# Groups of four share q and k, a block of two scores, four attends and two scores, softmax written over q and k: one edit of a four-layer graph network on Trainium2

## The chip, the cores and the metric

The kernel runs on one core of one Trainium2 chip, all in 32-bit floats. The metric is the device time of one launch in microseconds (us). The engines are named as the profile names them: PE is the matrix engine (PEld its weight loads), DVE the vector engine, ACT the scalar engine, POOL the general-purpose engine, and SP the engine that issues most DMAs. Each engine runs its own instructions in the order in which they were written down.

## The reference

There are 128 independent graphs ("batches") of 128 nodes with 512 features each, one shared 128x128 adjacency, and four layers, each followed by a residual and a layer norm. Cut to what matters:

```python
x = layernorm(x + (adj @ x) @ W0 + bias0)                    # layer 0
h = x @ W1                                                   # layer 1
e = leaky_relu(s1[:, None] + s2[None, :]) * adj              # s1, s2: h times two vectors
x = layernorm(x + elu(softmax(e) @ h + beta * h))
pre = A[:, :, None, :] + (C - A)[:, :, :, None]              # layer 2: A = adj @ x, C = A + b
x = layernorm(x + max(relu(pre), axis=-1))
q, k, v = split(x @ w_qkv)                                   # layer 3: 8 heads of 64
attn = softmax(where(adj == 0, -inf, q @ k.T * 64**-0.5))
o = (attn @ v) @ w_proj + b_proj
x = layernorm(x + o + layernorm(o) * gamma + beta3)
```

## The kernel before, in words

All weights stay in SBUF. Every batch is one 128x512 tile `xb` (nodes on the partitions), changed in place from its load to its store, with 16 such tiles (`BUFS["x"]`).

**The planner.** The program text is not written engine by engine. Each batch is a Python generator (`batch(i)`), and so are the side jobs of a group; each asks with `use(engine, work, names)` for a stretch of an engine, with an estimated duration and the buffers it needs. `Plan.run` simulates the engines and always emits next the request that could start earliest; ties go to `follow`, then `urgent`, then the lower rank (the older batch). The order so found is each engine's order on the chip. Buffers are taken in rotation: PSUM has five banks `mm` and three banks `tr`.

**Layers 0 to 2** of a batch: `mixed` (L231) multiplies the tile by the adjacency and turns it at once (L236, into a `tr` bank), ACT copies it out (L246), `product` (L224, L228) multiplies by W0, DVE adds (L643), a layer norm follows, then two logits per node (L650); `attention1` builds the attention of layer 1 for two batches, a second `mixed` and `product` apply it, DVE and ACT do the ELU (L666 to L671); one product with the adjacency (L678) and a maximum (L681) do layer 2.

**Layer 3** goes by groups, here of `G = 2` batches. `features` (L608) turns the tile with a DVE transpose (L692) and a trip through DRAM, into the group's buffer `xT` (two of these). When both batches are there, `query_key` (L507) runs four times per group: it multiplies two 128-column pieces of the weights with the group's `xT`, 256 columns wide (L519), and ACT or DVE copies the two pieces into the group's buffer `qkT` (L527, L529; three of these). `values` (L593) multiplies for v, at a low rank (`i + LATER`).

`tiled` (L536) is the block in which PE changes its tiling. It is emitted when q and k of a group are complete and the softmax rows of the group before it have come back. It holds the *scores* of its own two batches (L554: per batch 16 matmuls that contract over 64 rows, two at a time on the two halves of the array) and then the *attends* of the group before (`attends`, L582: 16 matmuls per batch that write 64 columns each). It asks for four `mm` banks, two `tr` banks, two `pr` and two `oT` buffers at once. After it, `batch` adds the mask (L706, out of the `mm` banks into `pr`), takes the maximum (L713), the exponentials on ACT (L717), the division (L723, L724), a 32x32 transpose into `pt` (L727), and a trip through DRAM into a buffer `prT` (L252, L256), which the attends read. The attended result is copied to `oT` (L749), multiplied by w_proj (L765, shown as L228), and `usual` (L762) does the rest: bias (L769), two layer norms, store.

The last 8 batches (`TAIL`) don't use the common block: their scores are emitted one batch at a time and their attends by pairs. The last 8 batches (`AHEAD`) also have their ranks lowered by 8. Batches 125 and 126 use `late` (L786), which puts part of the layer norms on ACT and stores from ACT's queue. Batch 127 uses `last` (L820): two column halves of the projection in one `mm` bank (L831), then DVE (L852, L853), one add on POOL of the whole tile (L221), the two layer norms and two half stores.

At the start `adjacency` (L348) clears a tile on DVE and multiplies it nine times (L355), then waits for the adjacency to land and transposes it (L360).

Each 32-bit `nc.tensor.matmul` appears in the trace as two MATMUL instructions, so a `product` is eight of 512 columns; a `nc.tensor.transpose` appears as one.

Of the kernel before, what the change touches and what calls it, by code (L numbers as in the profile page):

```python
# [15 lines left out]
P = 128  # L16
D = 512
K = D // P
G = 2
# [11 lines left out]
    "x": 16, "yT": 4, "z": 2, "e": 2, "et": 1, "eT": 2, "ex": 2, "xT": 2, "v": 6, "qkT": 3,  # L31
    "pr": 2, "pt": 1, "xt": 2, "prT": 2, "oT": 2, "o": 2,
}
AHEAD = 8
TAIL = 8
# [10 lines left out]
class Plan:  # L46

# [37 lines left out]
    def step(self, r, value):  # L85

        for want in iter(lambda: r["chain"].send(value), None):
            if not isinstance(want, Event):
                r["want"] = want
                self.requests.append(r)  # L90
                return
            if want.left:
                want.chains.append(r)
                return
            r["ready"], value = max(r["ready"], want.at), None
# [31 lines left out]
def gnn_stack_kernel(  # L127
# [62 lines left out]
    def mean_rstd_act(src, total):  # L190

        yield use("DVE", 0.15, follow=True)
        nm = small.tile([P, 1], F32, name="nm")
        nc.vector.tensor_scalar(nm, total, -1.0 / D, None, op0=ALU.mult)
        b = yield use("ACT", 1.2, "yT")
        square = buf([P, D], "yT")
        var = small.tile([P, 1], F32, name="var")
        nc.scalar.activation(square, src, AF.Square, bias=nm, accum_out=var)  # L198
        give(b)
        ve = small.tile([P, 1], F32, name="ve")  # L200
        nc.scalar.activation(ve, var, AF.Identity, bias=eps, scale=1.0 / D)
        return nm, (yield from root(ve, follow=True))
# [14 lines left out]
    def pool_add(dst, other, event, after=None):  # L217
        if after:
            yield after
        yield use("POOL", 1.4)  # L220
        nc.gpsimd.tensor_tensor(dst, dst, other, op=ALU.add)  # L221
        done(event)
# [8 lines left out]
    def mixed(xb, nodes, first=False):  # L231
# [6 lines left out]
        if first:  # L238

            yield use("DVE", 0.35, late=0.0)  # L240
            nc.vector.tensor_copy(yT[:, : K // 2], p[:, : K // 2])  # L241
            yield use("ACT", 0.05, urgent=True)
            nc.scalar.copy(yT[:, K // 2 :], p[:, K // 2 :])
        else:
            yield use("ACT", 0.6, urgent=True)
            nc.scalar.copy(yT, p)  # L246
# [16 lines left out]
    eps = const.tile([P, 1], F32, name="eps")  # L263
    nc.gpsimd.memset(eps, EPS)
# [40 lines left out]
    def loads():  # L305
# [14 lines left out]
        slot = yield use("SP", 1.0, "pr")  # L320
        matrix(w1_sb, w1)
        a_sb = buf([P, H, P], "pr").rearrange("p (s k) f -> p s (k f)", s=2)
# [24 lines left out]

    def adjacency():  # L348

        yield use("DVE", 0.1)  # L350
        nc.vector.memset(maskb, 0.0)
        b0 = yield use("PE", 2.0, "tr")
        p = bank([P, K, P], "tr")
        for i in range(9):
            nc.tensor.matmul(p[:, i % K, :], maskb, maskb, start=True, stop=True)  # L355
        give(b0)
        yield adj_in
        b0 = yield use("PE", 0.3, "tr", late=0.2, urgent=True)
        p = bank([P, K, P], "tr")
        nc.tensor.transpose(p[:, 0, :], adj_sb, ident)  # L360
        yield use("DVE", 0.3)
        nc.vector.tensor_copy(adjT, p[:, 0, :])
        give(b0)
        done(adj_ready)
# [35 lines left out]
    class Group:  # L400


        def __init__(self):
            self.s = small.tile([P, G, 2], F32, name="s")
            self.logits = [Event(2) for _ in range(G // 2)]
            self.attention = [Event() for _ in range(G // 2)]
            self.turned, self.qk = Event(G), Event(K)
            self.rows, self.attended = ([Event() for _ in range(G)] for _ in range(2))
            self.scored = [Event() for _ in range(G)]
            self.heads, self.o, self.prT, self.sc = {}, {}, [], {}  # L410
# [7 lines left out]

    groups = {}

    def group(g):
        if g not in groups:
            groups[g] = Group()
            for h in range(G // 2):
                plan.start(attention1(groups[g], h), g * G + 2 * h - (AHEAD if g * G >= NB - AHEAD else 0))
            for n in range(K):
                plan.start(query_key(groups[g], n // 2 * 2 + K * (n % 2)), g * G + n / K - (AHEAD if g * G >= NB - AHEAD else 0))


            rank = g * G - (AHEAD if g * G >= NB - AHEAD else 0)  # L430
            if g * G < NB - TAIL:
                plan.start(tiled(groups[g], groups.get(g - 1)), rank)
            else:
                for b in range(G):
                    plan.start(tiled(groups[g], None, (b,)), rank)
            if g * G >= NB - TAIL - G:
                for bs in ((0, 1),) if g * G < NB - G else ((0,), (1,)):
                    plan.start(attend(groups[g], bs), rank)
# [68 lines left out]
    def query_key(gr, c):  # L507
# [3 lines left out]
        if gr.qkT is None:  # L511
            bp, gr.slot["qkT"] = got
            gr.qkT = buf([P, 2 * K, G * P], "qkT")
        else:
            bp = got
        p = bank([P, 2, G * P], "mm")
        for j in range(2):
            for k in range(K):
                nc.tensor.matmul(  # L519
                    p[:, j, :], wqkv_sb[:, k, (c + j) * P : (c + j + 1) * P], gr.xT[:, k, :],  # L520
                    start=(k == 0), stop=(k == K - 1),
                )
        gr.read("xT", G + K)
        yield use("ACT" if c < K else "DVE", 0.69, urgent=True)
        dst = gr.qkT[:, c : c + 2, :]
        if c < K:
            nc.scalar.mul(dst, p, HD**-0.5)  # L527
        else:
            nc.vector.tensor_copy(  # L529
                dst.rearrange("p j (b c r) -> p (j b) c r", b=G, c=Q),  # L530
                p.rearrange("p j (b r c) -> p (j b) c r", b=G, c=Q),
            )
# [3 lines left out]
    def tiled(gr, before, bs=range(G)):  # L536
        yield gr.qk
        if before:
            for b in range(G):
                yield before.rows[b]  # L540
        n = len(bs)
        got = yield use(
            "PE", 0.25 + 0.88 * n + (0.88 * G + 0.15 if before else 0),
            lambda: ("mm", "mm", "pr") * n + ("tr", "oT") * (G if before else 0),
            late=0.0, urgent=True,
        )

        for b in bs:
            ps_b = [bank([P, K, P], "mm") for _ in range(2)]
            nodes = slice(b * P, (b + 1) * P)  # L550
            for c in range(K):
                for j in range(2):
                    rws = slice(j * HD, (j + 1) * HD)
                    nc.tensor.matmul(  # L554
                        ps_b[j][:, c, :], gr.qkT[rws, c, nodes], gr.qkT[rws, K + c, nodes],
                        start=True, stop=True,
                    )
            gr.read("qkT", G)
            gr.sc[b] = ps_b, got[:3]
            got = got[3:]  # L560
        if before:
            attends(before, range(G), got)

        for k, b in enumerate(bs):
            done(gr.scored[b], 0.15 - 0.88 * (n - 1 - k) - (0.88 * G + 0.3 if before else 0.15))

    def attend(gr, bs):
        for b in bs:
            yield gr.rows[b]
        slots = yield use(  # L570
            "PE", 0.25 + 0.88 * len(bs), lambda: ("tr", "oT") * len(bs), late=0.0, urgent=True
        )
        attends(gr, bs, slots)

    def attends(gr, bs, slots):
        for n, b in enumerate(bs):
            valued, prT, bt = gr.heads.pop(b)
# [9 lines left out]
            give(bt)  # L587
            give(valued.slot)
            gr.o[b] = p, slots[2 * n], slots[2 * n + 1]
        for b in bs:  # L590
            done(gr.attended[b], 0.2)

    def values(i, gr, event):  # L593
        b = i % G
        yield gr.turned
        bp = yield use("PE", 3.46, "mm", late=0.2)
# [3 lines left out]
        bv = yield use("ACT", 0.6, "v", urgent=True)  # L600
# [3 lines left out]
        gr.read("xT", G + K)  # L604
# [21 lines left out]
    def batch(i):  # L626
        g, b = divmod(i, G)
        h = b // 2
        yield loaded[i]
        gr, xb = group(g), xs[i]  # L630
# [58 lines left out]

        bt = yield use("DVE", 0.71, "xt")  # L690
# [11 lines left out]
        bpr = slots[2]  # L702
        for j in range(2):
            yield use("DVE", 0.69, urgent=True)
            pr = pr if j else buf([P, H, P], "pr")
# [9 lines left out]
        for j in range(H):  # L715
# [14 lines left out]
        give(bpr)  # L730
# [4 lines left out]
        got = yield use("SP", 0.5, lambda: () if gr.prT else ("prT",) * G, late=4.0)  # L735
        gr.prT = gr.prT or got
        bt = gr.prT.pop()
        prT = buf([P, Q, H * S], "prT")
        from_rows(prT, scratch)
        prT = prT.rearrange("p a (h s) -> p h a s", h=H)  # L740

        yield valued
        gr.heads[b] = valued, prT, bt
        done(gr.rows[b])
        yield gr.attended[b]
        p, ba, bo = gr.o.pop(b)
        yield use("ACT", 0.6, urgent=True)
        oT = buf([P, K, P], "oT")
# [3 lines left out]
        yield from (last if i == NB - 1 else late if i >= NB - 3 else usual)(  # L752
            i, xb, oT, bo, biased
# [8 lines left out]
    def usual(i, xb, oT, b_oT, biased):  # L762
# [3 lines left out]
        give(b_oT)  # L766
        bo = yield use("DVE", 0.69, "o", urgent=True)
        o = buf([P, D], "o")
# [11 lines left out]
        give(bo)  # L780
# [5 lines left out]
    def late(i, xb, oT, b_oT, biased):  # L786

        bp = yield use("PE", 3.46, "mm", late=0.2)
        p = product(lambda k: oT[:, k, :], lambda k: wproj_sb[:, k, :])
        give(b_oT)  # L790
        bo = yield use("DVE", 0.77, "o", urgent=True)
        o = buf([P, D], "o")
# [135 lines left out]
```

## Time and profile before

| | |
|---|---|
| median of 3 runs | 3264.58 us (3263.59 to 3264.89) |
| the profiled execution's own time | 3264.25 us |
| its span, first to last instruction | 3262.2 us |
| PE | 14,627 MATMUL, 3248.3 us busy |
| DVE | 2637.5 us busy, 81% of the span |
| ACT, POOL | 36% and 29% |
| mean granted PE clock | 0.999 |

The span is cut by the profile into rows by source line. A row has a busy time, the mean duration of one instruction and the idle time of its engine just before it with its releaser. For PE the mean duration of one instruction (593 ns for 128x512) is longer than the distance between two, as they are pipelined; distances are read from the timeline, where a run of equal matmuls has a start and a count, and the next run's start ends it.

### The profile page before, as it was taken

The page shows a single profiled execution, that of the slowest core. Times are in us where ns is not written, and L with a number is a line of the kernel's source. Part 1 is how long each engine was busy: PE and PEld are TensorE (multiplying, and loading weights), DVE is VectorE, ACT ScalarE, POOL GpSimd, SP SyncE. Part 2 cuts the span into 40 slices and gives each one's busy share as a digit, 9 for nine tenths or more (in the row PEclk, how much of TensorE's full clock was granted, in tenths as well). Part 3 has the DMA queues.
Part 4 walks back from the last instruction along what each step waited for, and adds up shares of the span by engine and source line. Part 5 has one row for each costly group of instructions (what it writes and reads, how often), then busy time and mean ns, then how long its engine had stood idle before and what let it go on. Part 6 is the DMA issues. An engine that isn't in the chain of part 4 may idle for free.

```text
span 3262.2 us, 43758 instructions
## 1 busy us (share of the span) xinstructions
PE 3248.3 (100%) x14627; PEld 2064.6 (63%) x14627; DVE 2637.5 (81%) x5656; ACT 1187.4 (36%) x3471; POOL 960.8 (29%) x1032
## 2 busy tenths in 40 slices
PE   9999999999999999999999999999999999999998
PEld 5666666665666656666566666665666656666665
DVE  7888788888887888888878888788887888788776
ACT  2433334333343333433424333243333333333333
POOL 3323232322322323223232232223322232223212
PEclk9999999999999999999999999999999999999999
DMA  4323323333223323233232332323323233223332
GB/s 165 84 82 98 102 81 91 103 87 94 96 75 104 98 82 101 73 101 100 81 105 72 97 104 77 108 74 95 105 72 108 80 92 102 75 89 96 89 113 81
DMA packets 469904, 304.47 MB, mean 93 GB/s; under 512 B 319280, under 2 KB 401584, under 8 KB 469680
## 3 DMA queue, kind: packets, MB, share of 16 engines
q1 hardware_dynamic: 469248, 300.90, 30.6%
q8 instruction: 116, 1.90, 0.2%
q14 instruction: 108, 0.88, 0.1%
q10 hardware_dynamic: 432, 0.79, 0.1%
HBM read 158.93 MB, written 142.67 MB: 92 GB/s over the span
## 4 chain that ended last, share of the span: by engine, by line
PE 100%; DVE 0%; ACT 0%; issue 0%; POOLq 0%; POOL 0%; DVEq 0%
PE mm L228 54%; PE mm L519 27%; PE tr L236 7%; PE mm L554 4%; PE tr L582 4%; PE mm L678 3%; PE tr L355 0%; PE mm L831 0%; DVE ex L867 0%; PE tr L394 0%; DVE st L853 0%; ACT yT L198 0%; DVE o L852 0%; DVE x L806 0%; DVE ex L802 0%
## 5 line engine op out<-in xcount | busy, mean ns | idle before, releaser
L228 PE MATMUL mm<-w_sb,yT 128*128 128x512 f32 x2048 | 908.0, 593 | 0.5 <-DVE yT L241 0.5
L519 PE MATMUL mm<-xT,wqkv_sb 128*128 128x256 f32 x4096 | 898.6, 379 | 0.0
L187 POOL TENSOR_TENSOR rstd<-ve,neghalf 128x1 f32<-128x1 f32 x640 | 457.2, 715 | 1420.2 <-DVE ve L181 1167.7
L519 PEld LDWEIGHTS mm<-xT,wqkv_sb 128*128 128x128 f32 x4096 | 777.3, 190 | 137.7 <-issue 29.8
L228 PEld LDWEIGHTS mm<-w_sb,yT 128*128 128x128 f32 x2048 | 384.0, 190 | 455.8 <-issue 445.1
L228 PE MATMUL mm<-wqkv_sb,xT 128*128 128x512 f32 x1024 | 460.2, 593 | 0.0
L228 PE MATMUL mm<-wproj_sb,oT 128*128 128x512 f32 x1016 | 447.0, 592 | 0.0
L717 ACT ACTIVATE pr<-pr,nmx 128x128 f32<-128x128 f32 x1024 | 396.3, 389 | 42.5 <-DVE nmx L713 41.3
L173 DVE BATCH_NORM_STATS2 st<-x 128x6 f32<-128x512 f32 x509 | 347.4, 683 | 25.3 <-ACT x L686 21.8
L228 PEld LDWEIGHTS mm<-wproj_sb,oT 128*128 128x128 f32 x1016 | 191.9, 190 | 231.4 <-issue 224.6
L228 PEld LDWEIGHTS mm<-wqkv_sb,xT 128*128 128x128 f32 x1024 | 188.3, 190 | 206.5 <-issue 203.4
L527 ACT ACTIVATE qkT<-mm 128x512 f32<-128x512 f32 x128 | 76.4, 597 | 628.7 <-PE mm L519 628.7
L221 POOL TENSOR_TENSOR x<-x,bias_sb 128x512 f32<-128x512 f32 x128 | 166.0, 1303 | 439.2 <-PE tr L236 429.8
L246 ACT COPY yT<-tr 128x512 f32<-128x512 f32 x255 | 149.4, 586 | 286.1 <-PE tr L236 285.8
L210 ACT ACTIVATE x<-x,nmr,rstd 128x512 f32<-128x512 f32 x256 | 205.5, 807 | 124.4 <-DVE nmr L208 120.4
L221 POOL TENSOR_TENSOR x<-x,o 128x512 f32<-128x512 f32 x128 | 178.3, 1393 | 218.9 <-DVE o L769 213.5
L221 POOL TENSOR_TENSOR x<-x,beta_sb 128x512 f32<-128x512 f32 x128 | 166.2, 1300 | 218.2 <-DVE xt L692 215.7
L666 ACT ACTIVATE ex<-mm 128x512 f32<-128x512 f32 x128 | 76.2, 596 | 346.5 <-PE mm L228 345.8
L650 DVE SCALAR_TENSOR_TENSOR scr<-x,wa_rows 128x512 f32<-128x512 f32 x256 | 186.0, 727 | 15.6 <-ACT x L210 10.8
L717 ACT ACTIVATION_READ_ACCUMULATOR pr<-pr,nmx 128x1 f32 x1024 | 192.8, 188 | 0.0
L706 DVE TENSOR_TENSOR pr<-mm,maskb 128x512 f32<-128x512 f32 x256 | 162.0, 682 | 28.8 <-PE mm L554 28.8
L724 DVE TENSOR_TENSOR pr<-pr,rs 128x1024 f32<-128x1024 f32 x128 | 161.8, 1264 | 4.4
(89 smaller groups left out, 3499.4 us busy)
## 6 DMA issues: line engine op xcount, KB each, us to landing
p_d<-pt SPq DMA_DIRECT2D x128, 512.0 KB
prT<-p_d SPq DMA_DIRECT2D x128, 512.0 KB
x_d<-xt SPq DMA_DIRECT2D x128, 256.0 KB
xT<-x_d SPq DMA_DIRECT2D x512, 64.0 KB
x<-in_x SPq DMA_DIRECT2D x127, 256.0 KB
out<-x SPq DMA_DIRECT2D x125, 256.0 KB
z<-s_d SPq DMA_DIRECT2D x64, 128.0 KB
e_d<-et SPq DMA_DIRECT2D x64, 128.0 KB
```

Source lines behind the costliest of these rows:

```text
L173: nc.vector.bn_stats(st, src)
L187: nc.gpsimd.tensor_tensor(rstd, ve, neghalf, op=ALU.pow)
L210: nc.scalar.activation(xb, xb, AF.Identity, bias=nmr, scale=rstd)
L221: nc.gpsimd.tensor_tensor(dst, dst, other, op=ALU.add)
L228: nc.tensor.matmul(p, lhs(k), rhs(k), start=(k == 0), stop=(k == K - 1))
L236: nc.tensor.matmul(p[:, k, :], xb[:, k * P : (k + 1) * P], nodes, start=True, stop=True)
L246: nc.scalar.copy(yT, p)
L519: nc.tensor.matmul(p[:, j, :], wqkv_sb[:, k, (c + j) * P : (c + j + 1) * P], gr.xT[:, k, :], start=(k == 0), stop=(k == K - 1),)
L650: nc.vector.scalar_tensor_tensor(scr, xb, 1.0, wa_rows[:, j, :], op0=ALU.mult, op1=ALU.mult, accum_out=gr.s[:, b, j : j + 1],)
L706: nc.vector.tensor_tensor(pr[:, j * K : (j + 1) * K], sc[j], maskb[:, None, :].to_broadcast([P, K, P]), op=ALU.add,)
L717: nc.scalar.activation(pr[:, j, :], pr[:, j, :], AF.Exp, bias=nmx[:, j : j + 1], accum_out=sums[:, j : j + 1],)
L724: nc.vector.tensor_tensor(pr, pr, rs[:, :, None].to_broadcast([P, H, P]), op=ALU.mult)
```

## The change

- `G` becomes 4. The first 29 groups ("quads", batches 0 to 115) have four batches; the last twelve batches make six groups of two (`PAIRS = 6`). `query_key` on a quad runs eight times with one 128-column piece each, 512 columns wide; on a pair it stays as it was. `xT` and `qkT` are twice as large, with two of each.
- `tiled` on a quad emits the scores of two batches, the attends of the four batches of the quad before (three at once, as there are three `tr` banks, and the fourth behind them), and the scores of the other two. Pairs emit scores per batch and attends per pair.
- The buffers `pr`, `prT`, `oT` and `o` are gone. The masked scores and the softmax of a batch are written over its q and k in `qkT`, and so are the turned rows that come back from DRAM. The attended result and then `o` are written over v. `qkT` is given back after the group's attends, v after the last use of `o`. `x` has 18 tiles (was 16), `v` 8 (was 6).
- `values` takes its v buffer together with PE. `early(i)` lowers the ranks of the last 14 batches by 8 (`LAST = 14`).
- `late` is gone: batches 125 and 126 use `usual`. `last` puts its halves in two `mm` banks and adds them on POOL half by half.
- At the start, ten transposes of the identity take the place of the nine products of zeros, with two more after the adjacency's transpose and two more after the first `mixed`. The DVE clear is gone.

```diff
-G = 2
+G = 4
+PAIRS = 6
-    "x": 16, "yT": 4, "z": 2, "e": 2, "et": 1, "eT": 2, "ex": 2, "xT": 2, "v": 6, "qkT": 3,
-    "pr": 2, "pt": 1, "xt": 2, "prT": 2, "oT": 2, "o": 2,
+    "x": 18, "yT": 4, "z": 2, "e": 2, "et": 1, "eT": 2, "ex": 2, "xT": 2, "v": 8, "qkT": 2,
+    "pt": 1, "xt": 2,
-AHEAD = 8
-TAIL = 8
+LAST, AHEAD = 14, 8
...
+    def fill(n):
+        for i in range(n):
+            nc.tensor.transpose(idle[0][:, i % K, :], ident, ident)
     def adjacency():
-        yield use("DVE", 0.1)
-        nc.vector.memset(maskb, 0.0)
         b0 = yield use("PE", 2.0, "tr")
-        p = bank([P, K, P], "tr")
-        for i in range(9):
-            nc.tensor.matmul(p[:, i % K, :], maskb, maskb, start=True, stop=True)
-        give(b0)
+        idle.append(bank([P, K, P], "tr"))
+        fill(10)
...
     def query_key(gr, c):
-            gr.qkT = buf([P, 2 * K, G * P], "qkT")
+            gr.qkT = buf([P, G, 2 * K, P], "qkT")
-        p = bank([P, 2, G * P], "mm")
-        for j in range(2):
+        n = gr.chunks
+        p = bank([P, n, gr.size * P], "mm")
+        for j in range(n):
             for k in range(K):
                 nc.tensor.matmul(
-                    p[:, j, :], wqkv_sb[:, k, (c + j) * P : (c + j + 1) * P], gr.xT[:, k, :],
-                    start=(k == 0), stop=(k == K - 1),
+                    p[:, j, :], wqkv_sb[:, k, (c + j) * P : (c + j + 1) * P],
+                    gr.xT[:, k, : gr.size * P], start=(k == 0), stop=(k == K - 1),
                 )
...
-    def tiled(gr, before, bs=range(G)):
+    def tiled(gr, before, bs):
         yield gr.qk
+        waiting = list(range(before.size)) if before else []
+        for b in waiting:
+            yield before.rows[b]
+        for n in range(0, len(bs), 2):
+            now, then = bs[n : n + 2], waiting[: BUFS["tr"]]
+            got = yield use(
+                "PE", 0.1 + 0.88 * len(now) + 0.15 + 0.87 * len(then),
+                lambda: ("mm", "mm") * len(now) + ("tr",) * len(then),
+                late=0.0, urgent=True, follow=n > 0,
+            )
...
+            for b in now:
+                score(gr, b, got[:2])
+                got = got[2:]
+            if then:
+                attends(before, then, got)
...
+            waiting = waiting[len(then) :]
+            while waiting:
+                got = yield use("PE", 0.88, "tr", late=0.0, follow=True)
+                attends(before, waiting[:1], [got])
+                waiting = waiting[1:]
...
     def attends(gr, bs, slots):
-            give(bt)
-            give(valued.slot)
+            gr.read("qkT", gr.size)
...
     def values(i, gr, event):
-        bp = yield use("PE", 3.46, "mm", late=0.2)
+        bp, bv = yield use("PE", 3.46, lambda: ("mm", "v"), late=0.2)
...
+        pr = gr.qkT[:, b]
...
+        prT = pr.rearrange("p h n -> p (h n)")
+        from_rows(prT.rearrange("p (a f) -> p a f", a=Q), scratch)
...
+        oT = valued.v.rearrange("p (k n) -> p k n", k=K)
         nc.scalar.copy(oT, p)
...
-        yield from (last if i == NB - 1 else late if i >= NB - 3 else usual)(
+        yield from (last if i == NB - 1 else usual)(
...
+        def multiply():
+            for h, columns in enumerate(halves):
+                bp = yield use("PE", 1.73, "mm", late=0.0, follow=h > 0)
+                p = bank([P, D // 2], "mm")
...
+            nc.vector.tensor_tensor(o[:, columns], p, bproj_sb[:, columns], op=ALU.add)
+            nc.vector.bn_stats(st[:, h], o[:, columns])
+            give(bp)
+            plan.start(pool_add(xb[:, columns], o[:, columns], added, biased, 0.7), i)
```

## The prediction

> **What bounds the kernel now.** I read the page's totals first, then PE's waits, then the timeline around one `tiled` block, then both ends of the span.
>
> ```profile
> span 3262.2 us, 43758 instructions
> ...
> PE 3248.3 (100%) x14627; PEld 2064.6 (63%) x14627; DVE 2637.5 (81%) x5656; ACT 1187.4 (36%) x3471; POOL 960.8 (29%) x1032
> ```
>
> PE is never free. Its whole list of waits is three, 2.0 us, all in the first 8 us:
>
> ```profile
> PE tr L355 <- DVE maskb L351: 1.1, 1, 1.1
> PE mm L228 <- DVE yT L241: 0.5, 1, 0.5
> PE tr L236 <- DVE adjT L362: 0.4, 1, 0.4
> ```
>
> So the span is a head, the sum of the distances between PE's matmuls, and a drain after the last one (3250.1 us by start and distance). Only what changes one of the three counts. Distances come from the timeline (start us, busy us, instruction, count): the next run's start ends a run. First a usual block, then one near the end:
>
> ```profile
> 1009.85 3.60 PE L228 MATMUL mm<-w_sb,yT 128*128 128x512 f32 x8
> 1013.38 2.06 PE L554 MATMUL mm<-qkT 64*128 64x128 f32 x32
> 1015.36 1.97 PE L582 MATMUL tr<-prT,v 128*64 128x128 f32 x32
> 1017.26 2.05 PE L236 MATMUL tr<-adjT,x 128*128 128x128 f32 x16
> 1019.15 3.62 PE L519 MATMUL mm<-xT,wqkv_sb 128*128 128x256 f32 x16
> 1022.61 7.03 PE L228 MATMUL mm<-wproj_sb,oT 128*128 128x512 f32 x16
> 1029.47 10.52 PE L519 MATMUL mm<-xT,wqkv_sb 128*128 128x256 f32 x48
> ...
> 3203.81 3.60 PE L228 MATMUL mm<-wproj_sb,oT 128*128 128x512 f32 x8
> 3207.34 1.16 PE L554 MATMUL mm<-qkT 64*128 64x128 f32 x16
> 3208.43 1.97 PE L582 MATMUL tr<-prT,v 128*64 128x128 f32 x32
> 3210.33 1.16 PE L554 MATMUL mm<-qkT 64*128 64x128 f32 x16
> 3211.42 3.70 PE L228 MATMUL mm<-wqkv_sb,xT 128*128 128x512 f32 x8
> ```
>
> Two facts are in there. L228 goes at 429.2 ns per 512 columns (1022.61 to 1029.47 is 16 of them), and L519 at 215.8 ns per 256 (48 in 10.36 us over its run). And a change of tiling costs time: eight L228 take 3.43 us undisturbed but 3.53 before scores. Instruction by instruction the distances around the blocks are the same everywhere: into scores +0.094 on the last full matmul; a run of scores has 0.102 on its first pair (213 for 112 ns) and 0.097 on its last; a run of attends 0.050 and 0.100 on a pair of 109; the first full matmul afterwards +0.104. A block of two scores and two attends thus carries 0.547 us besides its matmuls. The second block above is already the new shape, scores-attends-scores, and carries 0.094+0.199+0.150+0.199+0.104 = 0.746.
>
> **The change, part by part.**
>
> *Fewer changes of tiling.* Before, by the order of PE's runs: 59 common blocks, 4 lone pairs of scores (0.397 each), 4 lone pairs of attends (0.348), one scores-attends-scores: 32.3+1.6+1.4+0.7 = 36.0 us. After: the first quad's four scores 0.4, 28 blocks of the new shape 20.9, the last quad's attends as two pairs 0.7, six groups of two at 0.745 each 4.5: 26.5. Gain 9.5 us. The twelve last batches in twos are dearer than quads, which is counted. Lone runs that meet (as in the second block) would add up to 1 us.
>
> *Query and key at 512 columns.* 116 batches lose 16 MATMULs each: 1856 pairs of 256 become one of 512, at 2x215.83-429.17 = 2.5 ns: gain 4.6 us. The products are the same size and the weight loads stay covered (190 ns of load per 429). ACT and DVE copy as many columns as before.
>
> *What moves off PE's path.* Mask, maximum, exponentials, division, transpose, both DRAM trips and the three DVE or ACT copies keep their sizes and engines; only the tile they write differs. I cost this at nothing: DVE is 81% busy under a PE that is 100% busy. Were that cover gone it would be paid in waits, next.
>
> *The waits that it adds.* (a) The fourth attend needs the `tr` bank of the first, which ACT must have copied out: `oT` takes 0.59 us on ACT (L749), and between the end of attend one and the start of attend four lie two attends, 1.75 us. With 0.3 us to get through PE and at most an ACT instruction in the way (0.81), it fits. Behind it in PE's order stand the last two scores, and everything else. (b) These need four of five `mm` banks, so three of the first four masked (L706, 0.682 each, 2.05 us) and the product before the block evicted (0.69): 2.74 us of DVE. It has from 1.2 us after the scores' start (in the block shown DVE's first mask began at 1014.57) to 5.5, where the attends end: 4.3 us. A DVE instruction under way (up to 1.26, the division) leaves 0.3. It fits, narrowly. (c) q and k of quad g+2 wait for the attends of quad g, as `qkT` now lives through the softmax and there are two. A quad is 3262.2/32 = 101.9 us of PE; its eight query-key products are 27.5 and the block 7.4, so 35 after the release it could score. (d) The rows of quad g must return in the same time: per batch DVE works 2x0.682+1.205+0.193+1.264+1.236 = 5.26 us, 21 for four; DVE does other work for 60% of the time, so 53 us, and in the trace rows follow their score by 25 us with one pair in flight, transfers included. (e) v is held to the end of `o`; outputs followed attends by 15 to 25 us, some 40 with four in a row, which leaves 60 for four values of 3.4. All under 102 us, and 18 instead of 16 batches in flight are 50 us more for the group's wait. So PE should stay full. What each would cost if late is below. On SP's queue nothing is added but two earlier loads and the stores of 125 and 126, which leave ACT's; the from-DRAM transfer no longer waits for a `prT` tile.
>
> *The head.* The real work starts when the adjacency lands:
>
> ```profile
> 1.05 4.16 PE L355 MATMUL tr<-maskb 128*128 128x128 f32 x18 [1.05 <-DVE maskb L351]
> 5.05 0.27 PE L360 MATMUL tr<-ident,adj_sb 128*128 128x128 f32 x1
> ```
>
> The 18 multiplications of zeros go at 213 ns, and what follows at 111: the full clock came 4.0 us after PE's first instruction, just in time. The ten transposes can start when the identity is there (POOL ends it at 1.33) and last 2.1 us, to 3.6, with a gap until 4.8.[...] By the row (4.0 us after whatever comes first) the change costs nothing.[...] No transposes at a cold PE stand in this trace. I take 0.8, as the gap makes even counted transposes weaker than the row's; ends 0 and 2.8.[...]
>
> *The drain.* It is 12.1 us, from 3250.1 to 3262.2:
>
> ```profile
> 3250.34 0.42 DVE L852 TENSOR_TENSOR o<-mm,bproj_sb 128x256 f32<-128x256 f32 x1 [2.63 <-PE mm L831]
> 3251.75 1.26 POOL L221 TENSOR_TENSOR x<-x,o 128x512 f32<-128x512 f32 x1 [1.85 <-DVE o L852]
> 3254.33 0.75 DVE L806 SCALAR_TENSOR_TENSOR x<-ex,rstd,x 128x512 f32<-128x512 f32 x1
> 3255.19 0.74 DVE L873 SCALAR_TENSOR_TENSOR x<-ex,rstd,x 128x512 f32<-128x512 f32 x1
> ```
>
> The first half's add waited for the whole bank; with two banks it and its statistics (0.9 us) go under the second half. The POOL add of the whole tile (1.26) stood before the root of batch 127; half of it will. Without batch 126's DVE work in between, L873 could start near 3252.5 instead of 3255.19: 2.7 us. But 126 on `usual` needs 4.8 us of DVE, where `late` needed 2.8, and it lands in the same stretch. I take 1.7, ends 0 and 2.7.
>
> **Sum** against the profiled execution: 3264.25-9.5-4.6+0.8-1.7 = 3249.3; that execution was 0.3 below the median, so 3249.6 us.
>
> **The rivals.**
> - *The block breaks up.* If the planner finds no bank for the fourth attend, or for the second scores, it puts a product in between: scores after a product instead of after attends cost 0.198 more, and attends in two runs 0.348. Over 28 blocks 5.5 or 9.7 us of the 14.1 go: 3255 to 3260. For it: all three `tr` and four of five `mm` are asked for. Against: (a) and (b). 10%.
> - *PE starves at the end.* The last twelve batches in twos have shorter chains of PE work to hide a softmax behind, and 125 and 126 lean on DVE. Before, PE had no wait there. 3 to 8 us: 3252 to 3258. 10%.
> - *Slower: the second scores stand in the block.* If DVE's masks come late, PE waits in order, once per quad. 14.1 us over 28 blocks is 0.50 us each: beyond this the gain is gone, and with a division and a transpose ahead of the evictions (1.26+1.24+2.74 = 5.2 in 4.3) it is 0.9 us, and the time 3249.6+25 = 3275. For it: DVE at 81%, and a burst of four outputs follows each block. Against: the 0.3 us of room in the usual case, and masks are urgent. 5%.
> - *The change doesn't do it*: if switches didn't depend on order, only 4.6 us and the drain would stay, 3259. The second block shown speaks against it. 2%.
>
> **How the numbers follow.** The forecast as above, with clock and drain at either end, 73%: 3246.5 to 3253. The rivals take the range to 3259; below 3246 nothing in the parts reaches. What a measurement can tell from no change is 0.2%, 6.5 us, so faster means below 3258. Slower than 3271 is the third rival alone. Faster 0.88, same 0.08, slower 0.04.
>
> **What would show it.** PE has 14627-1856-4 = 12767 MATMULs; L519's row splits into 1856 of 512 and 384 of 256 columns; the blocks read 32, 64, 32 in the timeline with 0.746 us besides; PE's waits stay a few us in the head; the first product's distances are 429 ns (or 853 if the clock is late); L852's first half starts before PE ends. If PE shows waits on L706 or L749, or many more than the 35 to 41 runs of scores followed by a full matmul that the new order has, I was wrong on the block; if they lie after 3100 us, on the end.

## The result, and the profile after

The changed kernel takes 3252.30 us (median of six runs, 3251.55 to 3252.77) against 3264.41 us: 12.1 us less, a ratio of 0.9963 (95% interval 0.9950 to 0.9976). The forecast was 3249.6. The profiled execution was the quickest of the six, 3251.55 us, with a span of 3249.8 us against 3262.2.

The totals on the changed kernel's page:

```profile
span 3249.8 us, 40319 instructions
...
PE 3233.9 (100%) x12767; PEld 1713.2 (53%) x12767; DVE 2669.2 (82%) x5671; ACT 1186.4 (37%) x3469; POOL 954.7 (29%) x1032
```

L535 from its groups kept apart by shape (busy us, mean ns of one, idle before):

```profile
L535 PE MATMUL mm<-xT,wqkv_sb 128*128 128x512 f32 x1856 | 804.1, 592 | 0.0
```

The counts are those forecast: 12,767 MATMULs, 1856 of them query-key products of 512 columns. PE's waits, the whole list (total us, times, longest):

```profile
PE tr L353 <- POOL ident masks.py:199: 1.4, 1, 1.4
PE mm L706 <- ACT x L211: 0.8, 1, 0.8
PE mm L824 <- ACT v L776: 0.7, 1, 0.7
PE mm L229 <- ACT v L776: 0.7, 1, 0.7
PE mm L229 <- DVE yT L243: 0.3, 1, 0.3
```

Three of them are new and lie behind the head. None is inside a block, on L735 (the masks) or on a `tr` bank. (The lines are those of the changed kernel: its L706 is layer 2's product with the adjacency, not the mask that was L706 before. Its L776 is the copy of the attended result, L749 before; the two waits on it lie at 3228 and 3233 us, and it is the product with w_proj that waits, not an attend.) The block, from PE's timeline (start us, busy us, instruction, count):

```profile
1032.42 2.06 PE L590 MATMUL mm<-qkT 64*128 64x128 f32 x32
1034.40 3.71 PE L611 MATMUL tr<-qkT,v 128*64 128x128 f32 x64
1038.05 2.06 PE L590 MATMUL mm<-qkT 64*128 64x128 f32 x32
1040.03 12.28 PE L229 MATMUL mm<-wproj_sb,v 128*128 128x512 f32 x28
```

Two scores, four attends, two scores, with nothing between; 28 blocks read so. The fourth attend never waits for its bank: the 64 MATMULs of the four attends take 3.65 us, and 64 times their plain distance of 54.6 ns is 3.49; the other 0.15 is the surcharge of the run's two edges.

Taken apart by the distances between PE's matmuls, the two profiled executions differ by 12.4 us of span. (A wait is counted here as the distance beyond the plain one, so 0.97, 0.95 and 0.95 us, where the list above has the idle time of 0.8, 0.7 and 0.7. The drain is counted from the start of the last matmul.)

| part | forecast | found |
|---|---|---|
| changes of tiling | -9.5 | -9.6 (35.7 to 26.1) |
| merged query-key products | -4.6 | -4.6 |
| head, up to the first product with W0 | +0.8 | -1.1 (7.38 to 6.29 us) |
| PE's waits behind the head | 0 | +2.9 |
| drain after the last matmul | -1.7 | 0.0 (12.33 both) |
| sum | -15.0 | -12.4 |

### The profile page after: what moved, and what is told of

It reads as the page before. It is cut to its first block, busy times and chain, and to the rows that moved or that the text cites. A ratio compares the mean times of both kernels' runs of the same rounds, so it can differ in the third digit from the quotient of the medians.

```text
span 3249.8 us, 40319 instructions
## 1 busy us (share of the span) xinstructions
PE 3233.9 (100%) x12767; PEld 1713.2 (53%) x12767; DVE 2669.2 (82%) x5671; ACT 1186.4 (37%) x3469; POOL 954.7 (29%) x1032
## 4 chain that ended last, share of the span: by engine, by line
PE 99%; DVE 1%; POOL 0%; issue 0%; ACT 0%; POOLq 0%; DVEq 0%; ACTq 0%
PE mm L229 54%; PE mm L535 27%; PE tr L237 7%; PE mm L590 4%; PE tr L611 4%; PE mm L706 3%; DVE st L177 0%; POOL rstd L191 0%; PE tr L353 0%; DVE x L805 0%; POOL x L222 0%; DVE t L802 0%; DVE x L699 0%; DVE mv L183 0%; DVE v L795 0%
## 5 line engine op out<-in xcount | busy, mean ns | idle before, releaser
L535 PE MATMUL mm<-xT,wqkv_sb 128*128 128x512 f32 (+1 forms) x2240 | 888.7, 556 | 0.0
L535 PEld LDWEIGHTS mm<-xT,wqkv_sb 128*128 128x128 f32 x2240 | 425.1, 190 | 455.6 <-issue 424.9
L229 PE MATMUL mm<-wproj_sb,v 128*128 128x512 f32 x1016 | 444.4, 594 | 0.7 <-ACT v L776 0.7
L746 ACT ACTIVATE qkT<-qkT,nmx 128x128 f32<-128x128 f32 x1024 | 395.4, 390 | 40.1 <-DVE nmx L742 40.1
L222 POOL TENSOR_TENSOR x<-x,v 128x512 f32<-128x512 f32 x127 | 175.9, 1385 | 671.3 <-DVE v L795 669.5
L229 PEld LDWEIGHTS mm<-wproj_sb,v 128*128 128x128 f32 x1016 | 191.2, 190 | 235.6 <-issue 230.3
L544 ACT ACTIVATE qkT<-mm 128x512 f32<-128x512 f32 (+1 forms) x140 | 77.1, 560 | 554.8 <-PE mm L535 553.6
L735 DVE TENSOR_TENSOR qkT<-mm,maskb 128x512 f32<-128x512 f32 x256 | 163.7, 684 | 78.6 <-PE mm L590 78.5
L746 ACT ACTIVATION_READ_ACCUMULATOR qkT<-qkT,nmx 128x1 f32 x1024 | 193.7, 189 | 0.0
L630 ACT COPY v<-mm 128x512 f32<-128x512 f32 x128 | 74.8, 585 | 297.0 <-PE mm L229 296.5
```

Source lines behind the costliest of these rows:

```text
L229: nc.tensor.matmul(p, lhs(k), rhs(k), start=(k == 0), stop=(k == K - 1))
L535: nc.tensor.matmul(p[:, j, :], wqkv_sb[:, k, (c + j) * P : (c + j + 1) * P], gr.xT[:, k, : gr.size * P], start=(k == 0), stop=(k == K - 1),)
L735: nc.vector.tensor_tensor(pr[:, j * K : (j + 1) * K], sc[j], maskb[:, None, :].to_broadcast([P, K, P]), op=ALU.add,)
L746: nc.scalar.activation(pr[:, j, :], pr[:, j, :], AF.Exp, bias=nmx[:, j : j + 1], accum_out=sums[:, j : j + 1],)
```

## The experiments

All times are medians of 4 to 12 runs; each is compared with the changed kernel's 3252.30 unless said otherwise. The kernel before, timed beside every experiment, kept a median of 3264.1 to 3264.4.

**The block taken apart (e1_split).**

```diff
-            now, then = bs[n : n + 2], waiting[: BUFS["tr"]]
+            now, then = bs[n : n + 2], waiting[:2]
+            if n:
+                apart = Event()
+                done(apart, 6.0)
+                yield apart
...
-                late=0.0, urgent=True, follow=n > 0,
+                late=0.0, urgent=True,
...
-            while waiting:
+            while waiting and n + 2 >= len(bs):
```

> The changed kernel with each quad's block taken apart: two scores and two attends, then at least six planned us of other work, then the other two scores and two attends. By the order of PE's runs that makes 56 blocks of two scores and two attends plus the loose runs of the two ends, 37.3 us of tiling changes against 26.4 in the changed kernel. Theory (the time is PE's distances, and the block's gain is the tiling changes it saves): 10.9 us more than the changed kernel's 3252.3, so 3263, all of it at the edges of L590 and L611 runs. Rival (the gain came from groups of four and the freed buffers, not from the order inside the block): 3252 to 3254.

Measured: 3267.74 us, 15.4 more. The timeline has the two blocks per quad, with two products between, and one place of another kind:

```profile
1035.40 2.06 PE L594 MATMUL mm<-qkT 64*128 64x128 f32 x32
1037.39 1.97 PE L615 MATMUL tr<-qkT,v 128*64 128x128 f32 x32
1039.29 3.70 PE L229 MATMUL mm<-w_sb,yT 128*128 128x512 f32 x8
...
3168.65 1.09 PE L615 MATMUL tr<-qkT,v 128*64 128x128 f32 x16 [2.27 <-DMA qkT<-p_d]
3169.68 5.40 PE L535 MATMUL mm<-xT,wqkv_sb 128*128 128x256 f32 x16
```

In the spans the difference is 16.5. Of this 5.5 are PE's waits near the end and what follows one of them (a wait of 2.3 us for softmax rows, after which PE lost its full clock: the 16 MATMULs at 3169.68 take 5.24 us instead of 3.45), 0.5 head and drain, and 10.5 the edges of the blocks, where 10.9 was worked out. The order inside the block is worth what the distances say; the rival (no loss at all) is out. The other 5.5 us were not expected.

**Query and key 256 wide (e2_qk256).**

```diff
-        n = gr.chunks
-        p = bank([P, n, gr.size * P], "mm")
+        n = 2
+        p = bank([P, n, 2 * P], "mm")
...
-                    gr.xT[:, k, : gr.size * P], start=(k == 0), stop=(k == K - 1),
+                    gr.xT[:, k, 2 * h * P : 2 * (h + 1) * P], start=(k == 0), stop=(k == K - 1),
...
-            dst = gr.qkT[:, : gr.size, c + j, :]
+            dst = gr.qkT[:, 2 * h : 2 * h + 2, c + j, :]
```

> The changed kernel with the quads' query-key products 256 columns wide again (two 128-column pieces for two batches at a time), everything else kept, block order too. Theory (2.5 ns for every matmul that is not merged, 1856 of them): 4.6 us more, 3256.9; L535 all at 215.8 ns. ACT and DVE copy in twice as many instructions, some 15 us more DVE work, which lies under PE. Rival 1 (the width is nothing, weight loads and matmuls overlap): 3252.3. Rival 2 (the extra DVE instructions are felt, DVE being 82% busy): over 3260 with PE waits on DVE.

Measured: 3257.64, 5.3 more. The 4096 matmuls are back at 215.8 ns, with the blocks in the same order. The span is 5.8 longer: 4.6 is the merging, 0.8 one new wait of PE for layer 1's attention from DRAM, 0.3 the head. DVE's additional instructions (116 of them, 7.7 us by the two pages, where 15 were expected) show in no wait of PE.

**The head: the old products of zeros (e3_old_head), and nothing at all (e4_no_warm).** The edits put back the clear and the nine products of the kernel before, or leave out all of `fill`.

> The changed kernel with the old start: nine products of zeros behind a DVE clear, no transposes of the identity. Theory (the 18 matmuls at 213 ns held back the adjacency's transpose, which had landed by 3.5 us, and the full clock came in time either way): the first product with W0 starts near 7.4 instead of 6.29 us, 1.1 us more, 3253.4. Rival (transposes don't count towards the full clock, so the old start is the better one): full clock earlier than 4.9 us and no later first product, 3252 or less.

> The changed kernel with nothing on PE before the adjacency lands: no transposes of the identity at all. Theory (the ten transposes counted towards the full clock, which came 3.5 us after the first of them): full clock comes 3.4 to 4 us after the adjacency's transpose, so near 7 to 7.5 us instead of 4.9; the first mixed takes 0.8 us more and part of the first product runs at 853 ns a matmul; first product some 0.8 us later and 0.5 to 1 us longer, 3254. Rival (transposes don't count, the clock follows the real products alone): full clock at 4.9 us as with them, 3252.3.

Measured: 3252.95 and 3254.78. The first differs from the changed kernel by less than the runs spread (3252.11 to 3254.17 against 3251.55 to 3252.77), so that only the traces tell the two starts apart; the second is clear of it (3254.01 to 3255.23). First the changed kernel's start, then that without any warm-up:

```profile
1.36 2.40 PE L353 MATMUL tr<-ident 128*128 128x128 f32 x10 [1.36 <-POOL ident masks.py:199]
3.55 0.47 PE L362 MATMUL tr<-ident,adj_sb 128*128 128x128 f32 x1
6.29 3.70 PE L229 MATMUL mm<-w_sb,yT 128*128 128x512 f32 x8 [0.30 <-DVE yT L243]
```

```profile
3.69 0.45 PE L357 MATMUL tr<-ident,adj_sb 128*128 128x128 f32 x1 [3.69 <-DMA adj_sb<-in_adj]
7.12 5.95 PE L229 MATMUL mm<-w_sb,yT 128*128 128x512 f32 x8 [0.52 <-DVE yT L241]
12.90 1.28 PE L237 MATMUL tr<-adjT,x 128*128 128x128 f32 x10
```

The adjacency lands by 3.7 us. In the kernel before its transpose stood behind 18 matmuls of zeros until 5.05. In the changed kernel the MATMULs of 128 columns start 213 ns apart up to 4.4 us and 111 ns apart from 4.9 us on, 3.5 after the first transpose. Without the transposes the first product takes 5.78 us instead of 3.54. If the 2.24 us more are a stretch at half clock, this lasts 4.5 us and ends near 11.6: my estimate from these two numbers, where I had expected the full clock at 7 to 7.5 (the expectation's 853 ns a matmul is an estimate too, four times the 213 ns that 128 columns took). By itself this is one profile each. e8_last_first, which has the same start, decides: its first multiplication of data is

```profile
4.45 1.16 PE L237 MATMUL tr<-adjT,x 128*128 128x128 f32 x8
```

Its eight MATMULs take 1.16 us, like those at 5.71 us in the kernel before, of which the last seven start 111 to 112 ns apart; in e4_no_warm, with a single transpose ahead of them, they take 2.08. PE had done nothing but thirteen transposes until then, so transposes do count towards the full clock here. With the old start the same eight took 1.64 us this time, and the first product started at 8.00. When the full clock comes differs from run to run: a second profile of the unaltered changed kernel (e12_after_again, below) has 2.08 us for these eight instead of 1.38, and its first product at 7.22 us instead of 6.29. All eleven profiles with the ten transposes have it between 6.13 and 7.22 us, the two with the old start at 7.38 and 8.00. The gain of the new start thus lies between 0.2 and 1.9 us; the table's 1.1 is one draw of each.

**The drain: 125 and 126 on ACT again (e5_late), and 127 ahead of 126 on DVE (e8_last_first).** The first puts back `late` with v's tile for o. The second adds three lines:

```diff
         mv, rstd = yield from mean_rstd(o)
+        if i == NB - 2:
+            yield measured
         yield added
...
         mv, ve = mean_var(st)
+        done(measured)
         rooted, rstd = beside(root(ve, follow=True), i)
```

> The changed kernel with batches 125 and 126 finished on ACT as before the change (the old function for them, with v's tile for o), 127 as in the changed kernel. Theory (127's first half was ready at 3236.1 but stood behind 126's layer norms on DVE until 3239.07; this is why the drain stayed at 12.3 us): with 2 us less DVE work of 126 in the way the drain shrinks by 1.5 to 2.5 us, 3250.3. Rival (the drain is bound by 127's own chain of DVE and POOL steps after the second half): no change, 3252.3.

> The changed kernel where batch 126's second step (the scaled o and everything behind it on DVE) is written down only after batch 127's statistics of o, so that on DVE both halves of 127 come before it. Nothing is added or left out. Theory (the drain stayed at 12.3 us because 127's first half stood behind 126's layer norm on DVE until 3239.07): the first half's add starts near 3237.3, and the drain is 1 to 1.7 us shorter, 3251.0. Rival (126's work only moves behind, and its store ends last): 3252.3 or more.

The drain of the changed kernel, from the timeline (batch 126's L805, then 127's first half):

```profile
3238.41 0.75 DVE L805 SCALAR_TENSOR_TENSOR x<-t,rstd,x 128x512 f32<-128x512 f32 x1 [0.44 <-POOL rstd L191]
3239.07 0.42 DVE L839 TENSOR_TENSOR yT<-mm,bproj_sb 128x256 f32<-128x256 f32 x1
```

PE's last matmul starts at 3237.4: the first half's add, meant to go under the second half's products, comes after all of them. In e8_last_first (3251.19 us) the same add starts at

```profile
3237.18 0.41 DVE L843 TENSOR_TENSOR yT<-mm,bproj_sb 128x256 f32<-128x256 f32 x1
```

and the drain is 11.5 us instead of 12.3, 0.9 less where 1 to 1.7 was expected. e5_late shows the mechanism and its price: 3255.73 us, 3.4 more, although its drain is 9.9 us. ACT's queue had batch 125's square, which was waiting for DVE, ahead of the copy that PE needed:

```profile
3232.54 6.69 PE L243 MATMUL mm<-wproj_sb,v 128*128 128x512 f32 x8 [3.73 <-ACT v L792]
```

PE waited 3.7 us and lost its full clock: eight matmuls take 6.6 us instead of 3.4. My expectation saw the 2.4 us of drain and not the wait.

**Eight batches in twos instead of twelve (e6_pairs4), and 16, 17 or 20 batches in flight (e7_x16, e10_x17, e9_x20).** The edits are `PAIRS = 4`, and `"x": 16`, `17`, `20` in `BUFS` (the last on top of e8_last_first).

> The changed kernel with eight batches in twos at the end instead of twelve (one more quad). By the order of PE's runs 26.3 us of tiling changes instead of 26.4, and 64 more merged matmuls, 0.2 us. Theory (PE's distances alone): 3252. Rival (the last quad's softmax of four can no longer be hidden, which is what the twelve are for): PE waits of 3 to 10 us after 3100 us, 3255 to 3262, more where a wait is long enough to lose the full clock.

> The changed kernel with 16 batches in flight as before the change instead of 18. By PE's order 26.8 us of tiling changes. Theory (the longer life of q, k and v in groups of four leaves slack to spare; PE is full either way): 3252.7. Rival (groups of four need the two more tiles, since a group waits for its fourth batch): PE waits spread over the span, 3256 or more.

> The changed kernel with 17 batches in flight. 16 cost 57 us. By the order of PE's runs 27.0 us of tiling changes (26.4 with 18). Theory (a quad of four in scoring, four in attending and their outputs, and eight in layers 0 to 2 fill 16 tiles exactly; each tile beyond lets PE run ahead by one batch, 25 us, and the waits at the two ends go first): a good part of the 57 us is back, 3260 to 3275. Rival (a step at 18, the fourth batch of a group being the one that is late): 3295 or more.

> The kernel of e8_last_first with 20 batches in flight. By the order of PE's runs 26.8 us of tiling changes instead of 26.4. Theory (in the changed kernel PE waits three times after the head, 0.97 us at 123 us for want of ready batches and 0.95 twice at the last attends; only the first can be helped by more tiles): 0.97 less and 0.4 more, 3250.6. Rival (more tiles only move the work about): 3251.2 or more.

Measured: 3265.30, 3309.79, 3256.56 and 3274.10. In e6_pairs4, e7_x16 and e9_x20 my theory fell. All three have a PE wait of about 12 us near the end. In e6_pairs4 it reads (the last values, then the attends of batch 126):

```profile
3219.84 7.03 PE L229 MATMUL mm<-wqkv_sb,xT 128*128 128x512 f32 x16
3239.32 1.98 PE L611 MATMUL tr<-qkT,v 128*64 128x128 f32 x16 [12.46 <-DMA qkT<-p_d]
```

The last scores were emitted at 3214.3, their rows came 25 us later, and PE had 10.5 us of products left. In the changed kernel the last scores start at 3205.3 and PE has 19.5 us of work before it comes to the last two attends, so rows that take at most 21.5 us are covered. e9_x20 had 14 us left for rows that took 27.6, and e7_x16 14 for 28.0. The twelve batches in twos and the 18 tiles decide together how much work is left behind the last softmax. This is the larger part, not all: the rows were also slower in these three. In e6_pairs4 the request that brings batch 126's rows back left 21.1 us after the last scores had started, in the changed kernel 17.6; DVE had layer norms to do between masks and maximum. Nor does e9_x20 lose everything at the end. Of the 24.4 us by which its profiled execution is longer than the changed kernel's, 15.3 lie there by the distances, and 8.3 lie around 2840 us, with waits of 0.7, 2.7 and 1.1 us for tiles of the early layers; the other 3.8 are longer distances between matmuls, in an execution whose mean granted clock was 0.995 (0.999 in the changed kernel). Why 20 tiles bring that stretch no run shows.

That 16 tiles are worse than 17, and 17 than 18, has a second part. e7_x16's waits begin with

```profile
PE mm L706 <- ACT x L211: 15.7, 7, 4.5
PE mm L535 <- DMA s_d<-s: 13.0, 1, 13.0
PE tr L611 <- DMA qkT<-p_d: 12.3, 2, 12.0
```

The third is the one near the end; the second lies at 2936 to 2949 us, and its cause stays open. Of the first's seven, two are at the start (116 to 125 us); the other five, and one on z<-s_d (1.75 us at 486), come every 406 us (486, 893, 1300, 1707 us and on; 1.75 to 2.4 us each), which is 16 batches of 25.4: I read this as the kernel running out of ready batches once per turn of its 16 tiles. Further down the same list PE waits six times for masks (0.6 us at most) and twice for the copy of an attended result (0.5): with 16 tiles the narrow room of (a) and (b) is used up. With 17 tiles one wait of 2.3 us at 121 us and a few below 1 us remain, with 18 the one of 0.8; 17 gave back more of the 57 us than the 3260 to 3275 that I expected, and the rival of a step at 18 is out.

**The changed kernel again, and a last attempt (e12_after_again, e11_late_first).** The latter is e8_last_first with batch 126 alone finished by `late`, its square on ACT made to wait for the copy of 127's attended result.

> The changed kernel once more, unaltered, on the same chip and in the same rounds as e11_late_first, to compare the two. Theory: 3252.3, with its 12.3 us of drain.

> The kernel of e8_last_first where batch 126 alone is finished on ACT (the old function for it), its first square on ACT written down after the copy of 127's attended result, so that PE doesn't wait behind it, and its steps on DVE after 127's statistics. Theory (what is left of the drain is DVE's queue of both batches; ACT takes 2 us of it, and the wait of 3.7 us in e5_late came only from the square standing before the copy): L873's successor in the chain, the last scaling of 127, starts 1 us earlier than in e8_last_first, drain near 10.4 us, no wait of PE over 1 us, 3250.2. Rival (ACT and POOL steps of 126 are now the end): 3251.2 or more.

Measured: 3252.39 (3251.64 to 3253.71) and 3251.95 (3251.84 to 3252.81). e11_late_first has no long wait, but its drain is 12.0: 126's second square, root and scaling on ACT and POOL now end last, at 3246.9. The rival was right. The best version by its median is e8_last_first, 0.9959 of the kernel before (0.9945 to 0.9972); its 1.1 us on the changed kernel are within the spread of the runs (3250.51 to 3253.16), and what speaks for it is the drain that the profile shows.

## Why the prediction was right, and where it was off

*Changes of tiling.* Right, to 0.1 us, and shown by e1_split (10.5 us of edges for 10.9 counted): the edges of a block are constant, and counting blocks is enough. (33 runs of scores are followed by a full matmul, where 35 to 41 were counted: some lone runs at the end met.)

*Merging.* Right, shown by e2_qk256 (4.6 us for 4.6 counted).

*"So PE should stay full."* True in the steady state, for the stated reasons (a) and (b); the blocks have no wait. The arguments (c) to (e) allowed a margin that isn't there, and the room of (a) and (b) is gone with 16 tiles: I took the two additional tiles for a comfort of 50 us, and e7_x16 shows that the group of four needs them, at a price of 57 us. I had not worked out how many batches are held at one time.

*Waits.* The term that was mis-sized: 0 forecast, 2.9 us found, 0.97 at 124 us and 0.95 at each of the last two attends, where ACT's copy stands between an attend and its product with no other work left. The last two lie after 3100 us, where the prediction had set its sign of being wrong on the end: 1.9 us, a mild form of the second rival, which asked 3 to 8.

*The drain.* The step that failed is "I take 1.7". Two banks and half adds brought nothing, since DVE's queue had 126's layer norm in front; the prediction named that risk and valued it at 1 us instead of 1.7 or more. e8_last_first gets half of it back.

*The head.* Two errors: I read 4.8 us as the landing of the adjacency, where PE's own queue was the cause; and the late full clock, for which I charged 0.8 of a possible 2.8 us, was my estimate, which no trace had shown; in e8_last_first transposes alone brought it. The direction was wrong: +0.8 forecast, -1.1 found in the profile and at least -0.2 over all of them. This miss of 1 to 2 us on the good side was luck, and it hid part of the other two, 2.9 us of waits and 1.7 of drain; the 2.7 us between forecast and measurement are about what is left of the three.

*The rivals.* The block didn't break up and the second scores didn't wait. That switches don't depend on order is out too, by the 9.6 us found. That the end can starve is real: it happened in e6_pairs4, e7_x16 and e9_x20, not in the changed kernel.

## What to carry to other kernels

Where one engine has no waits, its time is a sum: read the distance of each kind of instruction and the surcharge of each change of mode, count both in the new order; for the two parts so forecast here it was good to 0.1 us. What such a sum can't give is whether the engine stays full; for that, count how many items are held at one time and how much work is left behind the last long latency, since what is missing there can cost more than the change brings: two tiles fewer cost 57 us here and one quad more at the end 13, where the change brought 12. An early half was worth something here only where the queue of the engine that takes it was free (0.9 us of drain in e8_last_first, nothing before).

## What was not expected of the hardware

A short wait can cost PE its full clock. After a wait of 2.3 us (e1_split) the next 16 MATMULs of 256 columns took 5.24 us instead of 3.45, and after one of 3.7 us (e5_late) the next eight of 512 took 6.6 instead of 3.4. The length alone doesn't decide. After another wait of 2.3 us, that of e10_x17 at 121 us, PE went on at full clock:

```profile
123.98 1.13 PE L706 MATMUL mm<-x,adjT 128*128 128x512 f32 x2 [2.28 <-ACT x L211]
124.94 3.60 PE L535 MATMUL mm<-xT,wqkv_sb 128*128 128x512 f32 x8
128.38 1.02 PE L706 MATMUL mm<-x,adjT 128*128 128x512 f32 x2
```

These eight take 3.44 us, 430 ns each. After 2.4 us in e7_x16 (at 1300 us) two of 512 columns take 0.97 us, as the first two here do (0.96). In the changed kernel the waits of 0.73 and 0.74 us at the last attends didn't lose it: the eight MATMULs after the first take 3.63 us with their edges. After the waits of about 12 us near the end of e6_pairs4, e9_x20 and e7_x16, followed by one of 0.73, the eight at that place took 6.16, 6.58 and 5.10 us. What tells the two waits of 2.3 us apart is not shown: no run varied when a wait comes or how much work lies around it.

And the full clock's arrival differs between runs of one program: the changed kernel's first product started at 6.29 us in one profile and at 7.22 in the other.
